# Attention scores of two heads in one matmul: L2's keys in blocks on zero, projected beside the heads

## The chip, the cores and the metric

The kernel runs on one core of a Trainium2 chip. The metric is the device time in microseconds from launch to end of that core. Everything is 32-bit float.

## The reference

A batch of 16 elements, each of 256 tokens by 256 features, goes through four blocks in a row, each steered by a vector `cond` of the element. L0 is a low-rank adapter. L1 is a bidirectional selective state-space layer (512 inner channels, 64 states, a scan over the 256 tokens in each direction) with a gated MLP. L2 and L3 are attention with a feed-forward layer each, L2 with 16 heads of 64 channels, L3 with 16 heads of 16. The change is in L2's attention:

```python
def _attention(x, W_qkv, W_out, b_out):
    qkv = x @ W_qkv
    q, k, v = jnp.split(qkv, 3, axis=-1)          # each (B, 256, 16 heads, 64)
    attn = jnp.einsum('bqhd,bkhd->bhqk', q, k) * DH ** (-0.5)
    attn = jax.nn.softmax(attn, axis=-1)
    out = jnp.einsum('bhqk,bkhd->bqhd', attn, v).reshape(Bq, Tq, INNER)
    return out @ W_out + b_out
```

## The kernel before, in words

The scan of L1 is one loop over 2048 states: 32 units (16 elements, two directions) of 64 states each. For every state, GpSimd (POOL) multiplies the input by a row of B into a buffer `h` (`drive`, L926, four states ahead), ScalarE (ACT) makes the decays (`decay`, L941), VectorE (DVE) scans `h` (`scan`, L969) and TensorE (PE) adds the result up by transposing `h` into `y` (`add_up`, L987, two states behind). The multiplication by a row of C is done by VectorE (L972, with a spread of C made on PE, L956) in five of eight states and by GpSimd (L976) in three of eight. There are eleven buffers `h` (`NH`). GpSimd can only write a buffer once PE has read what was in it.

Beside this loop two generators are advanced. `pend` does the front of the next unit (projections, L393 and L423, softplus, four GpSimd operations L452 to L461) and the back of the unit before, one yield per state. `other` runs `rest(b)`, which is the MLP of L1 and all of L2 and L3 of an element whose scan is done, one or two yields per state, three for two states. The instruction order on each engine is made by the builder, by and large in the order of the program; the engines run their own queues in order. The front and `rest` share two PSUM banks (`bank1`, `bank2`, tag `bank2`).

`rest` of fifteen elements lies beside the loop. For the last element the loop is over: the list `alone` is then filled, `bank2` goes round over six banks, and `rest` runs by itself as the tail of the program.

In L2, `rest` projects q (four times `dense`, two blocks of 128 channels each, L501), then k (the same, copied by ACT at L766), then v (four times at L774). Channels 0 to 63 of a block are an even head, 64 to 127 the odd one. Beside the loop, `heads2` goes over the 16 heads one by one:

- scores, per half of the tokens one matmul with 64 rows and 256 columns (L573);
- the row maximum over both halves (DVE, L578);
- two exponentials with the row sums (ACT, L582);
- one head later, four transposes (L592) and a copy `exT` by ACT (L596);
- for every second head, the product with v (L606) and a copy into `o` (L610).

In the tail, `heads2_alone` does two heads at a time. It puts the scores of the two heads alternately (L626; one head in rows 0 to 63, the other in 64 to 127), and has VectorE copy `exT` (L642).

L3's `heads3` has its keys on two tiles `kd[0]` and `kd[1]` of 128 by 4 by 256, in blocks of 32 rows on zero; small DMAs fill the blocks and the zeros are set once, at the start (L1121).

Weights come in a fixed order (`WEIGHTS`), two tiles in turn; `prefetch` asks for the one after next. All DMAs are issued on SyncE's queue (SP), in order: weights, the rows of B and C for the scan (`bb` of 512 KB for four states, `cb`), and the keys of L3.

Of the kernel before, what the change touches and what calls it, by code (L numbers as in the profile page):

```python
# [15 lines left out]
P = 128  # L16
B, T, D = 16, 256, 256
DC = D // P
# [36 lines left out]
def kernel(ctx: ExitStack, tc: tile.TileContext, a: dict, out: bass.AP):  # L55
# [24 lines left out]
    spill = dram.tile([P, 2, D], F32, name="spill")  # L80
    w3d = dram.tile([P, DC, 1024], F32, name="w3d")
    wvpd = dram.tile([P, 2048], F32, name="wvpd")

    at = {}
    row = 0
# [52 lines left out]
    def chunked(w):  # L138
        return w.rearrange("(c p) f -> p c f", p=P)
# [17 lines left out]
    def halves(t):  # L157
        return t.rearrange("p (c t) -> p c t", c=2)
# [116 lines left out]
    for t in maxima:  # L275
# [11 lines left out]
        )),  # L287
        ("l1w3", lambda w: ((w[:, 0:1024].rearrange("p (c f) -> p c f", c=IC), chunked(a["L1_cond_mlp_w3"])),)),
        ("wq", lambda w: ((w.rearrange("p (c f) -> p c f", c=DC), chunked(a["L2_cond_W_qkv"])[:, :, 0:1024]),)),
        ("wk", lambda w: ((w.rearrange("p (c f) -> p c f", c=DC), chunked(a["L2_cond_W_qkv"])[:, :, 1024:2048]),)),  # L290
        ("wv", lambda w: ((w.rearrange("p (c f) -> p c f", c=DC), chunked(a["L2_cond_W_qkv"])[:, :, 2048:3072]),)),
# [270 lines left out]
        yield  # L562
        prefetch()

    def heads2(q, k, v, o, rows):

        exs, exTs = {}, {}
        for i in range(16 + 3):
            if i < 16:
                sc = halves(bank2("sc"))  # L570
                base, ch = (i % 2) * 64, i // 2
                for t in range(NT):
                    nc.tensor.matmul(  # L573
                        sc[:, t], q[base : base + 64, ch, t * P : (t + 1) * P], k[base : base + 64, ch],
                        start=True, stop=True,
                    )
# [3 lines left out]
                ex = layers["soft"].tile([P, NT, T], F32, name="ex")  # L580
                for t in range(NT):
                    nc.scalar.activation(  # L582
                        ex[:, t], sc[:, t], AF.Exp, bias=nmax[:, t : t + 1],
                        accum_out=rows[:, t, i : i + 1],
                    )
                exs[i] = ex
            if 1 <= i < 17:
                ex = exs.pop(i - 1)
                pt = halves(bank2("pt"))
                for kt in range(NT):  # L590
                    for t in range(NT):
                        nc.tensor.transpose(  # L592
                            pt[:, kt, t * P : (t + 1) * P], ex[:, t, kt * P : (kt + 1) * P], ident
                        )
                exT = layers["soft"].tile([P, NT, T], F32, name="exT", bufs=3)
                nc.scalar.copy(exT, pt)  # L596
                exTs[i - 1] = exT
            yield
            if i % 2 and i >= 3:
                yield  # L600
                po = bank2("po")[:, :T]
                for h in (i - 3, i - 2):
                    exT = exTs.pop(h)
                    base = (h % 2) * 64
                    for kt in range(NT):
                        nc.tensor.matmul(  # L606
                            po[base : base + 64], v[:, kt, h * 64 : (h + 1) * 64], exT[:, kt],
                            start=(kt == 0), stop=(kt == NT - 1),
                        )
                nc.scalar.copy(o[:, (i - 3) // 2], po)  # L610
                yield

    def pair(name):

        return s3.tile([P, IC, T], F32, name=name, tag="h", bufs=NH).rearrange("p (j t) q -> p j t q", j=2)

    def heads2_alone(q, k, v, o, rows):

        exs, exTs = {}, {}
        for i in range(8 + 2):  # L620
            if i < 8:
                scs = [halves(bank2("sc")) for _ in range(2)]
                for t in range(NT):
                    for j in range(2):
                        rw = slice(64 * j, 64 * j + 64)
                        nc.tensor.matmul(  # L626
                            scs[j][:, t], q[rw, i, t * P : (t + 1) * P], k[rw, i], start=True, stop=True
                        )
                nmax = layers["soft"].tile([P, 2, NT], F32, name="nmax2")
                for j in range(2):  # L630
                    nc.vector.tensor_reduce(nmax[:, j], scs[j], AX.X, ALU.max, negate=True)
            if 1 <= i < 9:
                ex = exs.pop(i - 1)
                exT = pair("exT")
                for j in range(2):
                    pt = halves(bank2("pt"))
                    for kt in range(NT):
                        for t in range(NT):
                            nc.tensor.transpose(
                                pt[:, kt, t * P : (t + 1) * P], ex[:, j, t, kt * P : (kt + 1) * P], ident  # L640
                            )
                    nc.vector.tensor_copy(exT[:, j], pt)  # L642
                exTs[i - 1] = exT
            if i >= 2:
                exT = exTs.pop(i - 2)
                po = bank2("po")[:, :T]
                for kt in range(NT):
                    for j in range(2):
                        h = 2 * (i - 2) + j
                        nc.tensor.matmul(  # L650
                            po[64 * j : 64 * j + 64], v[:, kt, h * 64 : (h + 1) * 64], exT[:, j, kt],
                            start=(kt == 0), stop=(kt == NT - 1),
                        )
                nc.scalar.copy(o[:, i - 2], po)
            if i < 8:
                ex = pair("ex")
                for j in range(2):
                    for t in range(NT):
                        nc.scalar.activation(
                            ex[:, j, t], scs[j][:, t], AF.Exp, bias=nmax[:, j, t : t + 1],  # L660
                            accum_out=rows[:, t, 2 * i + j : 2 * i + j + 1],
                        )
                exs[i] = ex

    def heads3(q, k, v, oT):

# [27 lines left out]
        def values(g):  # L694
            ex = []
            for j in range(4):
                tag, n = (("ex", 2), ("exT", 3))[j // 2]
                ex.append(layers["soft"].tile([P, NT, T], F32, name="ex3", tag=tag, bufs=n))
# [31 lines left out]
    def rest(b):  # L730
# [24 lines left out]
        k = layers["pa"].tile([P, 8, T], F32, name="k")  # L755
        v = layers["pa"].tile([P, NT, 1024], F32, name="v")
        o = q
        w = weights("wq", DC)
# [2 lines left out]
            yield  # L761
        prefetch()
        offset(b, 0)
        w = weights("wk", DC)
        for m in range(0, 8, 2):
            nc.scalar.copy(k[:, m : m + 2], dense(w, hT, m, 2, DC))  # L766
# [274 lines left out]
    def late():  # L1041
# [168 lines left out]
```

## Time and profile before

| what | value |
| --- | --- |
| median of three runs | 7628.08 us (7628.05 to 7632.17) |
| the profiled execution, its own time | 7630.37 us |
| its span, first to last instruction | 7628.6 us |
| busy: DVE, POOL | 6886.1 us (90%), 6912.3 us (91%) |
| busy: PE, ACT | 6253.0 us (82%), 5370.7 us (70%) |
| moved by DMA | 675.87 MB, 26.0% of 16 engines' span |
| granted TensorE clock | 0.928 of full speed |

The loop takes nearly all of the span; the tail, the last element alone, begins a little after 7390 us. One element beside the loop takes some 454 us; its L2 heads are 88 us of these, and 26.6 us in the tail. A line of the profile names the line of the kernel, the engine, what is written and read, the count, the busy time and the mean of one, and what the engine waited for before it. A matmul in 32-bit float shows as two records, and records overlap.

### The profile page before, as it was taken

How to read it: one execution, taken by the hardware profiler on the slowest of the kernel's cores; microseconds unless marked ns; L12 is line 12 of the kernel's file. 1: busy time of each engine (PE TensorE's matmuls, PEld its weight loads, DVE VectorE, ACT ScalarE, POOL GpSimd, SP SyncE). 2: the span in 40 equal slices, each digit the busy share in tenths (PEclk: the TensorE clock that was granted, in tenths of full speed). 3: DMA queues.
4: the chain of work that ended last, by engine and by line, in shares of the span. 5: the costliest groups of instructions: out<-in, count | busy, mean ns of one | idle time of the engine just before them, and what ended most of it. 6: DMA issues, size and time to landing. Idle time of an engine off the chain costs nothing. (4 is left out here: it accounts for less than half of the span.)

```text
span 7628.6 us, 100211 instructions
## 1 busy us (share of the span) xinstructions
PE 6253.0 (82%) x35215; PEld 4947.6 (65%) x35215; DVE 6886.1 (90%) x6951; ACT 5370.7 (70%) x12013; POOL 6912.3 (91%) x2991
## 2 busy tenths in 40 slices
PE   6568888888888888888888888888888888888778
PEld 4456666666667666666666667666666666667655
DVE  3988998999999999999999999899999999999972
ACT  3567776777767777776777777777776777777653
POOL 3999999999999999999999999999999999999960
PEclk8679999999999999999999999999999999999999
DMA  4112232222322222232222222222232222222211
GB/s 167 52 60 93 85 103 73 92 90 87 108 79 96 79 95 94 92 103 73 85 100 86 100 86 97 78 92 93 87 105 78 92 85 96 94 92 92 72 64 49
DMA packets 331642, 675.87 MB, mean 89 GB/s; under 512 B 24724, under 2 KB 204032, under 8 KB 326784
## 3 DMA queue, kind: packets, MB, share of 16 engines
q1 hardware_dynamic: 331136, 669.44, 26.0%
q8 instruction: 278, 4.55, 0.2%
q14 instruction: 228, 1.87, 0.1%
HBM read 650.22 MB, written 10.75 MB: 87 GB/s over the span
## 5 line engine op out<-in xcount | busy, mean ns | idle before, releaser
L969 DVE TENSOR_TENSOR_SCAN h<-decay,h 128x512 f32<-128x512 f32 x4096 | 4735.2, 1204 | 271.5 <-ACT decay L941 189.3
L926 POOL TENSOR_TENSOR h<-dtx,bb 128x1024 f32<-128x1024 f32 x2048 | 4794.8, 2370 | 79.9 <-PE y L987 79.8
L987 PE MATMUL y<-ident,h 128*128 128x128 f32 x16384 | 2457.7, 296 | 836.8 <-POOL h L976 798.8
L987 PEld LDWEIGHTS y<-ident,h 128*128 128x128 f32 x16384 | 2083.4, 153 | 1216.4 <-POOL h L976 940.9
L941 ACT ACTIVATE decay<-dt,a_neg_bwd 128x255 f32<-128x255 f32 x4096 | 1814.5, 469 | 824.1 <-DVE h L969 777.0
L941 ACT ACTIVATE decay<-dt,a_neg_fwd 128x255 f32<-128x255 f32 x4096 | 1807.9, 471 | 641.1 <-DVE h L969 598.9
L976 POOL TENSOR_TENSOR h<-h,cb 128x1024 f32<-128x1024 f32 x768 | 1816.5, 2365 | 199.5 <-DVE h L969 172.0
L972 DVE TENSOR_TENSOR h<-h,cs 128x1024 f32<-128x1024 f32 x1280 | 1526.0, 1204 | 73.7 <-PE cs L956 62.9
L956 PE MATMUL cs<-ident,cT 128*128 128x128 f32 x2560 | 503.6, 290 | 88.5 <-DVE h L972 86.1
L956 PEld LDWEIGHTS cs<-ident,cT 128*128 128x128 f32 x2560 | 332.1, 146 | 163.4 <-DVE h L972 123.9
L573 PE MATMUL sc<-k,q 64*128 64x256 f32 x960 | 283.1, 417 | 17.7 <-ACT ex L582 17.0
L393 PE MATMUL pxz<-hTm,w_in 128*128 128x256 f32 x1024 | 275.8, 387 | 15.4 <-DVE maxima L683 12.3
L582 ACT ACTIVATE ex<-sc,nmax 128x256 f32<-128x256 f32 x480 | 222.1, 468 | 71.9 <-DVE nmax L578 69.1
L701 PE MATMUL scT<-qk,kd 128*128 128x256 f32 x984 | 248.8, 385 | 28.6 <-DVE qk L692 23.1
L680 PE MATMUL sc<-kd,qk 128*128 128x512 f32 x490 | 252.0, 621 | 14.2 <-DVE maxima L683 10.0
L596 ACT COPY exT<-pt 128x512 f32<-128x512 f32 x240 | 139.8, 583 | 162.7 <-PE pt L592 162.4
L423 PE MATMUL pdt<-xz,w_dt 128*128 128x256 f32 x1024 | 245.9, 383 | 0.0
L573 PEld LDWEIGHTS sc<-k,q 64*128 64x128 f32 x960 | 167.0, 193 | 99.8 <-ACT ex L582 32.9
L701 PEld LDWEIGHTS scT<-qk,kd 128*128 128x128 f32 x984 | 176.1, 190 | 58.3 <-ACT pr L429 24.9
L393 PEld LDWEIGHTS pxz<-hTm,w_in 128*128 128x128 f32 x1024 | 179.2, 193 | 43.2 <-DVE maxima L683 15.7
L423 PEld LDWEIGHTS pdt<-xz,w_dt 128*128 128x128 f32 x1024 | 189.4, 193 | 21.8
L578 DVE TENSOR_REDUCE nmax<-sc 128x2 f32<-128x512 f32 x240 | 162.1, 676 | 35.7 <-PE sc L573 35.5
(348 smaller groups left out, 7530.1 us busy)
## 6 DMA issues: line engine op xcount, KB each, us to landing
bb<-bd SPq DMA_DIRECT2D x512, 512.0 KB
cb<-bd SPq DMA_DIRECT2D x256, 384.0 KB
l2w<-in_L_cond_W_dram SPq DMA_DIRECT2D x32, 1024.0 KB
l3w<-in_L_cond_W_dram SPq DMA_DIRECT2D x32, 1024.0 KB
l1w<-in_L_cond_mlp_w_dram SPq DMA_DIRECT2D x48, 512.0 KB
w_in<-in_L_cond_fwd_in_w_dram SPq DMA_DIRECT2D x16, 1024.0 KB
w_dt<-_L_cond_fwd_xproj_w_dram SPq DMA_DIRECT2D x16, 1024.0 KB
w_in<-in_L_cond_bwd_in_w_dram SPq DMA_DIRECT2D x16, 1024.0 KB
```

Of the source, the lines that this page charges most:

```text
L393: nc.tensor.matmul(px[:, j], w_in[:, c, (m + j) * P : (m + j + 1) * P], hT[:, c], start=(c == 0), stop=(c == DC - 1),)
L423: nc.tensor.matmul(pp[:, j], w_dt[:, c, (m + j) * P : (m + j + 1) * P], xz[:, c], start=(c == 0), stop=(c == IC - 1),)
L573: nc.tensor.matmul(sc[:, t], q[base : base + 64, ch, t * P : (t + 1) * P], k[base : base + 64, ch], start=True, stop=True,)
L680: nc.tensor.matmul(sc, q[:, g, t * P : (t + 1) * P], kd[g % 2][:, 2 * i : 2 * i + 2], start=True, stop=True)
L701: nc.tensor.matmul(sc[:, kt], kd[g % 2][:, j, kt * P : (kt + 1) * P], q[:, g], start=True, stop=True)
L926: nc.gpsimd.tensor_tensor(h, st[u][4], bb.unsqueeze(1).to_broadcast([P, IC, T]), ALU.mult)
L941: nc.scalar.activation(dc[:, j, 1:T], st[u][3][:, c, when], AF.Exp, scale=a_neg[d][:, c, s : s + 1])
L956: nc.tensor.transpose(cs[:, i % 2, t * P : (t + 1) * P], st[u][1][:, t, s : s + 1].to_broadcast([P, P]), ident)
L969: nc.vector.tensor_tensor_scan(hv, dv, hv, 0.0, ALU.mult, ALU.add)
L972: nc.vector.tensor_tensor(h, h, c.unsqueeze(1).to_broadcast([P, IC, T]), ALU.mult)
L976: nc.gpsimd.tensor_tensor(h, h, c.unsqueeze(1).to_broadcast([P, IC, T]), ALU.mult)
L987: nc.tensor.matmul(ys[u][:, t, c * P : (c + 1) * P], h[:, c, t * P : (t + 1) * P], ident, start=(s == 0 and c == 0), stop=(s == NS - 1 and ...
```

## The change

The projection of k is no longer a stage of its own. `heads2` now also serves the tail, and `heads2_alone` is gone. It goes over 16 steps: a pair of heads `p` and a half of the tokens `t`. Before every second pair it projects two blocks of keys and writes each head's 64 rows into its own columns of `kd`, two copies by ACT. The rest of `kd` is zero, so that one matmul of 128 rows and 512 columns gives the scores of both heads for 128 tokens. One maximum, two exponentials (one per head) and four transposes follow as before; `exT` now holds a pair. As L3 needs zeros in other places of `kd`, both tiles are overwritten with zeros from DRAM before L2 and again after its heads (`blank`, a DMA of 512 KB each). The zeros are written to DRAM once. Weights of v now come before those of k.

```diff
+    def blank(g):
+        nc.sync.dma_start(kd[g], zeros.rearrange("p (j t) -> p j t", j=4))
...
-    def heads2(q, k, v, o, rows):
+    def heads2(w, hT, q, v, o, rows):
         exs, exTs = {}, {}
         for i in range(16 + 3):
+            p, t = i // 2, i % 2
+            if i == 0 or (i % 4 == 2 and i < 14):
+                g = 0 if i == 0 else i // 4 + 1
+                ps = dense(w, hT, 2 * g, 2, DC)
+                keys = kd[g % 2].rearrange("p (m j) t -> p m j t", m=2)
+                for j in range(2):
+                    rw = slice(64 * j, 64 * j + 64)
+                    nc.scalar.copy(keys[rw, :, j], ps[rw])
+                if g == 3:
+                    prefetch()
+                yield
             if i < 16:
+                keys = kd[(p // 2) % 2].rearrange("p (m j) t -> p m j t", m=2)
                 sc = halves(bank2("sc"))
-                base, ch = (i % 2) * 64, i // 2
-                for t in range(NT):
-                    nc.tensor.matmul(
-                        sc[:, t], q[base : base + 64, ch, t * P : (t + 1) * P], k[base : base + 64, ch],
-                        start=True, stop=True,
-                    )
-                nmax = layers["soft"].tile([P, NT], F32, name="nmax")
+                nc.tensor.matmul(sc, q[:, p, t * P : (t + 1) * P], keys[:, p % 2], start=True, stop=True)
+                nmax = layers["soft"].tile([P, 2], F32, name="nmax")
                 nc.vector.tensor_reduce(nmax, sc, AX.X, ALU.max, negate=True)
                 yield
...
             if 1 <= i < 17:
                 ex = exs.pop(i - 1)
+                p1, t1 = (i - 1) // 2, (i - 1) % 2
+                if t1 == 0:
+                    exTs[p1] = layers["soft"].tile([P, 2 * NT, T], F32, name="exT")
+                pt = bank2("pt").rearrange("p (n t) -> p n t", t=P)
+                for n in range(2 * NT):
+                    nc.tensor.transpose(pt[:, n], ex[:, n // NT, (n % NT) * P : (n % NT + 1) * P], ident)
+                (nc.vector.tensor_copy if alone else nc.scalar.copy)(exTs[p1][:, :, t1 * P : (t1 + 1) * P], pt)
...
-    def heads2_alone(q, k, v, o, rows):
...
+        for g in range(2):
+            blank(g)
         hT = yield from norm3(b, m_l2, 0)
...
-        w = weights("wk", DC)
-        for m in range(0, 8, 2):
-            nc.scalar.copy(k[:, m : m + 2], dense(w, hT, m, 2, DC))
-            yield
-        prefetch()
...
-        if alone:
-            heads2_alone(q, k, v, o, rows)
-        else:
-            yield from heads2(q, k, v, o, rows)
+        yield from heads2(weights("wk", DC), hT, q, v, o, rows)
+        yield
+        for g in range(2):
+            blank(g)
...
-            nc.gpsimd.memset(kd[j], 0.0)
+            if j == 0:
+                nc.gpsimd.memset(kd[j], 0.0)
+                nc.sync.dma_start(zeros, kd[j].rearrange("p j t -> p (j t)"))
```

More of the change, by code (lines that the diff above doesn't have):

```diff
@@ L82 @@
     wvpd = dram.tile([P, 2048], F32, name="wvpd")
+    zeros = dram.tile([P, 4 * T], F32, name="zeros")
     at = {}
@@ L289 @@
         ("wq", lambda w: ((w.rearrange("p (c f) -> p c f", c=DC), chunked(a["L2_cond_W_qkv"])[:, :, 0:1024]),)),
+        ("wv", lambda w: ((w.rearrange("p (c f) -> p c f", c=DC), chunked(a["L2_cond_W_qkv"])[:, :, 2048:3072]),)),
         ("wk", lambda w: ((w.rearrange("p (c f) -> p c f", c=DC), chunked(a["L2_cond_W_qkv"])[:, :, 1024:2048]),)),
-        ("wv", lambda w: ((w.rearrange("p (c f) -> p c f", c=DC), chunked(a["L2_cond_W_qkv"])[:, :, 2048:3072]),)),
         ("l2out", lambda w: ((w.rearrange("p (c f) -> p c f", c=8), chunked(a["L2_cond_W_out"])),)),
@@ L563, in feed_forward @@
         prefetch()
-    def heads2(q, k, v, o, rows):
+    def blank(g):
+        nc.sync.dma_start(kd[g], zeros.rearrange("p (j t) -> p j t", j=4))
+    def heads2(w, hT, q, v, o, rows):
         exs, exTs = {}, {}
         for i in range(16 + 3):
+            p, t = i // 2, i % 2
[9 more added lines that the diff above has]
+                yield
             if i < 16:
+                keys = kd[(p // 2) % 2].rearrange("p (m j) t -> p m j t", m=2)
                 sc = halves(bank2("sc"))
-                base, ch = (i % 2) * 64, i // 2
-                for t in range(NT):
-                    nc.tensor.matmul(
-                        sc[:, t], q[base : base + 64, ch, t * P : (t + 1) * P], k[base : base + 64, ch],
-                        start=True, stop=True,
-                    )
-                nmax = layers["soft"].tile([P, NT], F32, name="nmax")
+                nc.tensor.matmul(sc, q[:, p, t * P : (t + 1) * P], keys[:, p % 2], start=True, stop=True)
+                nmax = layers["soft"].tile([P, 2], F32, name="nmax")
                 nc.vector.tensor_reduce(nmax, sc, AX.X, ALU.max, negate=True)
                 yield
-                ex = layers["soft"].tile([P, NT, T], F32, name="ex")
-                for t in range(NT):
+                ex = layers["soft"].tile([P, 2, T], F32, name="ex")
+                for j in range(2):
                     nc.scalar.activation(
-                        ex[:, t], sc[:, t], AF.Exp, bias=nmax[:, t : t + 1],
-                        accum_out=rows[:, t, i : i + 1],
+                        ex[:, j], sc[:, j], AF.Exp, bias=nmax[:, j : j + 1],
+                        accum_out=rows[:, t, 2 * p + j : 2 * p + j + 1],
                     )
@@ L588, in heads2 @@
                 ex = exs.pop(i - 1)
[L589 to L597, printed above, removed]
+                p1, t1 = (i - 1) // 2, (i - 1) % 2
[5 more added lines that the diff above has]
+                (nc.vector.tensor_copy if alone else nc.scalar.copy)(exTs[p1][:, :, t1 * P : (t1 + 1) * P], pt)
             yield
@@ L601, in heads2 @@
                 po = bank2("po")[:, :T]
-                for h in (i - 3, i - 2):
-                    exT = exTs.pop(h)
-                    base = (h % 2) * 64
+                p1 = (i - 3) // 2
+                exT = exTs.pop(p1)
+                for j in range(2):
+                    h = 2 * p1 + j
                     for kt in range(NT):
                         nc.tensor.matmul(
-                            po[base : base + 64], v[:, kt, h * 64 : (h + 1) * 64], exT[:, kt],
+                            po[64 * j : 64 * j + 64], v[:, kt, h * 64 : (h + 1) * 64], exT[:, j * NT + kt],
@@ L608, in heads2 @@
                             start=(kt == 0), stop=(kt == NT - 1),
                         )
-                nc.scalar.copy(o[:, (i - 3) // 2], po)
+                nc.scalar.copy(o[:, p1], po)
                 yield
-    def pair(name):
-        return s3.tile([P, IC, T], F32, name=name, tag="h", bufs=NH).rearrange("p (j t) q -> p j t q", j=2)
-    def heads2_alone(q, k, v, o, rows):
[L619 to L663, printed above, removed]
@@ L696, in values @@
             for j in range(4):
-                tag, n = (("ex", 2), ("exT", 3))[j // 2]
-                ex.append(layers["soft"].tile([P, NT, T], F32, name="ex3", tag=tag, bufs=n))
+                if j < 2:
+                    ex.append(layers["soft"].tile([P, NT, T], F32, name="ex3", tag="ex"))
+                elif j == 2:
+                    two = layers["soft"].tile([P, 2 * NT, T], F32, name="ex3", tag="exT")
+                    ex += [two[:, :NT], two[:, NT:]]
                 sc = halves(bank2("scT"))
@@ L751, in rest @@
         prefetch()
+        for g in range(2):
+            blank(g)
         hT = yield from norm3(b, m_l2, 0)
         q = layers["pa"].tile([P, 8, T], F32, name="q")
-        k = layers["pa"].tile([P, 8, T], F32, name="k")
         v = layers["pa"].tile([P, NT, 1024], F32, name="v")
```

## Prediction, made before the changed kernel was run

> **What bounds the kernel now.** I read the page first, then busy time by stage, then who waited for whom in the stage that the change touches, then single instructions there and in the tail.
>
> ```profile
> PE 6253.0 (82%) x35215; PEld 4947.6 (65%) x35215; DVE 6886.1 (90%) x6951; ACT 5370.7 (70%) x12013; POOL 6912.3 (91%) x2991
> ...
> L969 DVE TENSOR_TENSOR_SCAN h<-decay,h 128x512 f32<-128x512 f32 x4096 | 4735.2, 1204 | 271.5 <-ACT decay L941 189.3
> L926 POOL TENSOR_TENSOR h<-dtx,bb 128x1024 f32<-128x1024 f32 x2048 | 4794.8, 2370 | 79.9 <-PE y L987 79.8
> ...
> L573 PE MATMUL sc<-k,q 64*128 64x256 f32 x960 | 283.1, 417 | 17.7 <-ACT ex L582 17.0
> ...
> L680 PE MATMUL sc<-kd,qk 128*128 128x512 f32 x490 | 252.0, 621 | 14.2 <-DVE maxima L683 10.0
> ```
>
> POOL (L926, L976) and VectorE (L969) carry the scan. POOL idles for little, and where it does, the multiply L926 waits for PE's transposes into y, which free an h buffer. POOL's work is not touched, so the loop gets shorter only where POOL idles less. One batch element as an example (46 us of L2's q, k, v; 88 us of its heads; the rest), then the two stages of the last element, which runs alone:
>
> ```profile
> 2012.00:2058.00 46.00, 42.82 (x225) 33.89 (x224) 39.91 (x37) 42.59 (x86) 41.40 (x18) 1.00 0.48 169
> 2058.00:2146.00 88.00, 70.97 (x446) 55.28 (x446) 80.56 (x79) 62.19 (x175) 87.55 (x39) 0.91 0.19 65
> 2146.00:2411.00 265.00, 224.61 (x1280) 178.08 (x1277) 253.52 (x262) 189.79 (x406) 250.48 (x109) 0.95 0.26 86
> 7416.00:7459.80 43.80, 39.18 (x138) 29.02 (x138) 3.54 (x6) 14.84 (x24) 0.00 (x0) 0.86 0.28 96
> 7459.80:7486.40 26.60, 25.38 (x193) 16.50 (x192) 20.39 (x33) 17.93 (x72) 0.00 (x0) 1.00 0.12 40
> ```
>
> Columns: stretch, length, busy PE, PEld, DVE, ACT, POOL, clock, DMA share, GB/s. In the heads POOL is full (87.55 of 88) and the others have room. In q, k, v it is the reverse: PE and ACT are at 93% and POOL loses 4.6 us. In the tail's heads PE is full (25.38 of 26.60). Who held POOL, in the waits of 2012 to 2146 and in POOL's, ACT's and PE's instructions in order of time:
>
> ```profile
> POOL h L926 <- PE y L987: 5.1, 3, 2.8
> ```
> ```profile
> 2046.83 2.37 POOL L926 TENSOR_TENSOR h<-dtx,bb 128x1024 f32<-128x1024 f32 x1 [2.78 <-PE y L987]
> ...
> 2055.68 2.36 POOL L926 TENSOR_TENSOR h<-dtx,bb 128x1024 f32<-128x1024 f32 x1 [1.83 <-PE y L987]
> 2058.49 2.36 POOL L926 TENSOR_TENSOR h<-dtx,bb 128x1024 f32<-128x1024 f32 x1 [0.45 <-PE y L987]
> 2060.80 2.36 POOL L976 TENSOR_TENSOR h<-h,cb 128x1024 f32<-128x1024 f32 x1
> ```
> ```profile
> 2044.64 1.99 PE L501 MATMUL dense<-hT,wk 128*128 128x256 f32 x8 [1.65 <-ACT k L766]
> ...
> 2051.12 3.60 PE L774 MATMUL pv<-wv,hT 128*128 128x512 f32 x8
> 2054.56 1.04 PE L987 MATMUL y<-ident,h 128*128 128x128 f32 x8
> ...
> 2058.55 1.13 PE L573 MATMUL sc<-k,q 64*128 64x256 f32 x4
> ```
> ```profile
> 7459.79 0.48 PE L626 MATMUL decay<-k,q 64*128 64x256 f32 x1
> 7459.79 0.48 PE L626 MATMUL sc<-k,q 64*128 64x256 f32 x1
> 7460.11 0.38 PE L626 MATMUL decay<-k,q 64*128 64x256 f32 x1
> 7460.11 0.38 PE L626 MATMUL sc<-k,q 64*128 64x256 f32 x1
> ```
>
> The transposes stand behind the twelve projections of q, k, v on PE's queue; and PE itself waits 1.65 us for a PSUM bank that ACT has yet to empty.
>
> **The change, part by part.** An f32 matmul leaves two records.
>
> *Scores in the loop.* By mean durations a pair of heads would fall from 8 x 417 = 3.3 us to 4 x 621 = 2.5 us. These overlap, so they are not costs. A head's four records of 256 columns span 1.13 us with the last at 0.38, so starts are some 0.21 to 0.25 apart; at L774, of 512 columns too, 8 records span 3.60 with the last at 0.59, so 0.43 apart. Per pair: 8 x 0.21 = 1.7 us before, 4 x 0.43 = 1.7 us after. Cost and gain 0: half of the new products are with zeros.
>
> *Where a rule speaks against it.* In the tail, records of the two heads start in the same hundredth (7459.79, 7459.79) and again 0.32 and 0.21 later: rows 0 to 63 and 64 to 127 work at once. The Trainium skill ("TensorE: Matmul & The Clock Gate", Part 3 on packing small matmuls) says that a matmul with few rows takes as long as one with 128, and that such matmuls in different row groups run at once; filling the rows with zeros throws that away. By the rule everywhere it would be 128 pairs x 0.85 = 109 us of PE. The loop's rows show four matmul records of one head alone, one after another, so nothing is lost there; I charge the tail only.
>
> *Tail.* Before: 3.1 us per pair of heads (scores begin at 7464.27, 7467.37, 7470.47, ...), of which 1.06 are scores. After: 1.71 + the same 2.04 = 3.75, so 8 x 0.65 = +5.2 us. The four key projections (7445.71 to 7452.61, 6.9 us) move and stay on PE: 0. Before the first score come two copies of the keys on ACT, 2 x 0.58 = 1.2, partly filled by the next projection: +1. The half-pair order leaves less between a score and its transposes: from a score's start to its second exponential's end it is 1.0 + 0.7 + 0.9 + hand-overs of 0.1 = 3.0 us, while PE has 0.85 + 0.5 + 0.85 = 2.2 without an output matmul between: bound 0 to 0.8 us per pair, 0 to 6; by the 0.3 us that L639 waits per pair now I take 2. Tail: **+8 us** (5 to 13).
>
> *Keys moved in the loop.* Four projections (8 records in some 1.73 us each, 6.9 in all) leave the stage where PE holds POOL and go into the heads, one before every second pair. Cover there: PE 71.0 + 6.9 of 88. If that cover were gone, they would cost what they cost now. In q, k, v, v takes k's place, so PE's work up to 2046.8 is as before and the wait of 2.78 stays. After it, PE has one key projection, two scores and a set of transposes (1.7 + 2.0 + 0.4 = 4.1 us) where v's four had 6.9; the 1.83 and 0.45 should go: 2.3 us. Late next is ACT: from 2048.7 to 2061.6 it has no gap (dtx to uu, 6.4 us, four copies of v 2.3), VectorE waits 3.0 for a decay, and L976 at 2060.80 began 0.3 us after its scan. In the new order two key copies, two exponentials and one exT (1.2 + 0.9 + 0.6) stand there for v's copies. So POOL, earlier, will wait for a scan instead; bound 0 to 2.3, I take half: **-1.1 us** per element, 15 elements, **-16 us**.
>
> *Copies on ACT.* A group of keys is written as two copies of 64 rows x 512 where one of 128 x 512 took 0.58; the row nearest is that one, and with the columns equal I take 0.58: +2.3 us per element. From below 0.3 each (rows counted) they would be free. Cover: ACT 62.2 of 88. Behind a copy that waits for its projection stand the decays, and VectorE for those; at the first group the score itself waits for the copies, and the y transposes stand behind it on PE. Charged 0 beyond what is above; without cover 15 x 2.3 = +35.
>
> *The blanks.* Four DMAs of 512 KB per element, on SP's queue, in front of bb, cb and weights. The page has 669 MB in 26% of the span: 3.0 us per MB, an estimated 1.6 us for each. A bb is asked for when its buffer comes free and used four multiplies later (9.5 us); L926 waited for PE in 79.8 of its 79.9 us, never for a DMA. Two blanks before a bb (3.1 us) stay under 9.5. What a blank waits for (the scores of the last pair, L3 of the element before) is three or more steps old. 0; if not covered, 6 us per element.
>
> *Rest.* The zero fill of one block (0.95 us on POOL) goes, before the loop, where POOL then idles 36.9 us: 0. One more turn of the generator per element moves all after it by two thirds of a state, 2.4 us, and adds no work; the last but one element ends at 7388 with the loop at 7392: 0. exT and ex sizes are the same in sum; l2w1 is fetched later, still some 25 us ahead of its use: 0.
>
> **Sum:** +8 - 16 = -8 on 7630.4 (the profiled execution; span 7628.6), 7622. That execution is 2.3 above the median of the three, 7628.1, so about **7620**.
>
> **The rivals.**
> 1. *No measurable change*, the sum above, 7600 to 7640 (within 15 us, 0.2%, about what a measurement can tell from none, for most of it). For it: POOL is full in the heads, the score's PE time is equal. Chance 0.42.
> 2. *All of POOL's wait for y goes*, as ACT keeps up: 5.1 x 15 = 76 less, 8 more: 7560. For: that wait is PE's. Against: the first 2.78 lies before the change of order. Chance 0.21.
> 3. *The keys block PE in the heads.* In the loop two PSUM banks serve scores, transposes, projections and the front's matmuls. Each projection waits for a bank that ACT must empty (1.65 us at 2044.64), in front of y. Four such waits, 6.6 us per element, less the two now seen in q and k (2.6): 4 x 15 = 60, with 8 for the tail 7696; half of it 7660. It decides once PE's lateness uses up the free h buffers, so that POOL waits for y within the heads. For: PE is in order, and ACT waits 11.8 us for transposes there already. Against: POOL shows almost no wait in these 88 us. Chance 0.37.
>
> That the matmuls get no cheaper is already in the sum; that the blanks delay bb is part of 3's upper end.
>
> **Numbers.** Faster by over 0.2%: nearly all of 2 and a quarter of 1: 0.30. Within: 0.32 from 1 and the edges. Slower: 3: 0.38. Range 7575 to 7690: half of 2 and the top of 3 left out.
>
> **What would show it.** L573 and L626 gone, score records of 128x512 at about 0.6 us; POOL's waits for y after v gone (right) or new ones inside the heads (rival 3); PE busy in a heads stage up by about 7 us, POOL full; the tail's heads with keys some 8 us longer than 6.9 + 26.6. L926 waiting for bb, or POOL less than 95% busy in the heads, would make it wrong.

## The result, and the profile after

The changed kernel is slower: a median of 7729.8 us (7723.2 to 7735.2, four runs) against 7628.1 us (7625.5 to 7632.2), a ratio of 1.013 with a 95% interval of 1.0118 to 1.0142. That is about 100 us more, where 8 us less had been forecast, and outside the range. The profiled execution took 7727.3 us, its span is 7725.5 us.

From the page of the changed kernel, the lines that answer to those of before. L885 is now POOL's multiply `drive`, L928 the scan, L935 POOL's multiplication by C, L589 L2's scores; L640 and L664 are L3's scores and their transposed counterpart.

```profile
PE 6169.6 (80%) x34703; PEld 4804.0 (62%) x34703; DVE 6886.6 (89%) x6951; ACT 5475.3 (71%) x12077; POOL 6911.8 (89%) x2990
...
L928 DVE TENSOR_TENSOR_SCAN h<-decay,h 128x512 f32<-128x512 f32 x4096 | 4746.0, 1211 | 291.1 <-ACT decay L900 163.9
L885 POOL TENSOR_TENSOR h<-dtx,bb 128x1024 f32<-128x1024 f32 x2048 | 4794.1, 2369 | 160.7 <-PE y L946 159.0
...
L664 PE MATMUL scT<-qk,kd 128*128 128x256 f32 x984 | 264.9, 401 | 83.1 <-DVE qk L652 65.1
...
L589 PE MATMUL sc<-kd,q 128*128 128x512 f32 x492 | 280.0, 653 | 26.9 <-ACT exT L608 16.3
...
L640 PE MATMUL sc<-kd,qk 128*128 128x512 f32 x490 | 255.9, 615 | 43.9 <-DVE maxima L643 43.8
```

Read the busy times first. POOL works 6911.8 us, before 6912.3; VectorE 6886.6, before 6886.1. So the 97 us of span are idle time of both. The wait of `drive` for PE's transposes into `y` has doubled, 79.9 to 160.7. And the two rows whose waits have grown most on PE are not L2's: they belong to L3. The change leaves L3's instructions as they are; it only gives the exponentials of `values` other buffers (two of a group's four heads share one), and the first two experiments show that this costs nothing. L640 waited 14.2 before and waits 43.9 now. L664 stood as L701 in the page before:

```profile
L701 PE MATMUL scT<-qk,kd 128*128 128x256 f32 x984 | 248.8, 385 | 28.6 <-DVE qk L692 23.1
```

Busy time by stage, after, for the element that the prediction took as its example, with the columns as there: q and v, then the heads with their keys, then the stage of L3's attention. The last two lines are the tail's two stages.

```profile
2027.00:2063.70 36.70, 33.11 (x169) 25.31 (x168) 35.47 (x34) 33.52 (x72) 32.41 (x15) 1.00 0.48 156
2063.70:2161.00 97.30, 79.64 (x483) 58.42 (x482) 84.68 (x83) 75.57 (x195) 95.76 (x42) 0.93 0.27 91
2268.90:2379.00 110.10, 96.88 (x548) 71.99 (x547) 104.33 (x108) 81.48 (x172) 100.42 (x44) 0.97 0.26 84
7509.10:7545.80 36.70, 32.06 (x104) 23.10 (x105) 3.54 (x6) 12.67 (x20) 0.00 (x0) 0.84 0.25 86
7545.80:7584.90 39.10, 38.45 (x193) 22.71 (x193) 21.35 (x33) 23.54 (x81) 0.00 (x0) 1.00 0.24 81
```

The stage of L3's attention of the same element before:

```profile
2249.90:2355.00 105.10, 95.91 (x551) 71.64 (x551) 103.51 (x108) 79.03 (x171) 100.42 (x44) 0.98 0.24 83
```

q, v and the heads take 36.7 + 97.3 = 134.0 us; q, k, v and the heads took 46.0 + 88.0 = 134.0. The changed part is neither faster nor slower in this element. L3's stage does the same work (POOL 100.42 us in 44 instructions both times) and takes 5.0 us longer: POOL idles 9.7 us of it where it idled 4.7. Averaged over fourteen elements in the middle of the loop, POOL idles 28.2 us per element against 21.6 before; 15 times the difference is 99 us. The loss is in the loop, and most of it is not where the change is.

Who held POOL in L3's stage, after and then before (each line: waits in total, times, longest):

```profile
POOL h L885 <- PE y L946: 7.2, 4, 3.8
POOL h L935 <- DVE h L928: 2.5, 1, 2.5
```
```profile
POOL h L976 <- DVE h L969: 2.9, 3, 1.3
POOL h L976 <- POOL h L926: 1.0, 1, 1.0
POOL h L926 <- PE y L987: 0.7, 1, 0.7
```

The longest wait, 3.78 us at 2331.77, and what PE did before it, in order of time:

```profile
2323.33 4.67 POOL L885 TENSOR_TENSOR h<-dtx,bb 128x1024 f32<-128x1024 f32 x2
2331.77 2.37 POOL L885 TENSOR_TENSOR h<-dtx,bb 128x1024 f32<-128x1024 f32 x1 [3.78 <-PE y L946]
```
```profile
2322.97 0.44 PE L651 MATMUL pm<-ident,maxima 128*128 128x128 f32 x2 [1.26 <-ACT pr L430]
2323.25 1.04 PE L946 MATMUL y<-ident,h 128*128 128x128 f32 x8
2324.12 0.38 PE L915 MATMUL cs<-ident,cT 128*128 128x128 f32 x2
2327.12 1.10 PE L664 MATMUL scT<-qk,kd 128*128 128x256 f32 x4 [2.62 <-DVE qk L652]
2328.06 1.89 PE L424 MATMUL pdt<-xz,w_dt 128*128 128x256 f32 x8
2329.79 1.03 PE L664 MATMUL scT<-qk,kd 128*128 128x256 f32 x4
2330.65 1.04 PE L946 MATMUL y<-ident,h 128*128 128x128 f32 x8
```

At the same place in the kernel before:

```profile
2303.24 0.38 PE L691 MATMUL pm<-ident,maxima 128*128 128x128 f32 x2
2303.45 1.25 PE L987 MATMUL y<-ident,h 128*128 128x128 f32 x10
2306.26 1.97 PE L701 MATMUL scT<-qk,kd 128*128 128x256 f32 x8 [1.55 <-DVE qk L692]
2308.06 0.82 PE L987 MATMUL y<-ident,h 128*128 128x128 f32 x6
```

In L3 PE spreads the maxima (`pm`), VectorE adds them to `qk`, and PE makes `scT` from it. PE is in order. Before, the chain came up with transposes in front of it, and 4.6 us lie between the starts of two groups of `y`. After, `pm` first waits 1.26 us for a PSUM bank that ACT must empty (`pr`, of the next unit's front), then `scT` 2.62 us for VectorE, and a product `pdt` of the front follows; the two groups of `y` start 7.4 us apart. POOL's buffer is late by 3.8 us. L3 and the next unit's front are the same instructions as before. What differs is how they lie against each other and against the scan: L3 comes later by one turn of the generator.

The example stands for the others. Over the fourteen elements, POOL waits for `y` in L3 for 7.3 us per element; before it was 0.3. A second, smaller growth lies where a forward unit starts: there POOL's `yg` (L470, in the back of the unit before) waits for VectorE for 4.0 us per element, before 2.4.

### The profile page after: what moved, and what is told of

It reads as the page before. It is cut to its first block, busy times and chain, and to the rows that moved or that the text cites. A ratio compares the mean times of both kernels' runs of the same rounds, so it can differ in the third digit from the quotient of the medians.

```text
span 7725.5 us, 99391 instructions
## 1 busy us (share of the span) xinstructions
PE 6169.6 (80%) x34703; PEld 4804.0 (62%) x34703; DVE 6886.6 (89%) x6951; ACT 5475.3 (71%) x12077; POOL 6911.8 (89%) x2990
## 5 line engine op out<-in xcount | busy, mean ns | idle before, releaser
L928 DVE TENSOR_TENSOR_SCAN h<-decay,h 128x512 f32<-128x512 f32 x4096 | 4746.0, 1211 | 291.1 <-ACT decay L900 163.9
L885 POOL TENSOR_TENSOR h<-dtx,bb 128x1024 f32<-128x1024 f32 x2048 | 4794.1, 2369 | 160.7 <-PE y L946 159.0
L946 PE MATMUL y<-ident,h 128*128 128x128 f32 x16384 | 2361.0, 288 | 733.9 <-POOL h L935 684.4
L946 PEld LDWEIGHTS y<-ident,h 128*128 128x128 f32 x16384 | 2008.6, 148 | 1152.8 <-POOL h L935 796.1
L900 ACT ACTIVATE decay<-dt,a_neg_bwd 128x255 f32<-128x255 f32 x4096 | 1837.3, 472 | 813.2 <-DVE h L928 757.6
L935 POOL TENSOR_TENSOR h<-h,cb 128x1024 f32<-128x1024 f32 x768 | 1815.5, 2364 | 187.7 <-DVE h L928 177.1
L664 PE MATMUL scT<-qk,kd 128*128 128x256 f32 x984 | 264.9, 401 | 83.1 <-DVE qk L652 65.1
L589 PE MATMUL sc<-kd,q 128*128 128x512 f32 x492 | 280.0, 653 | 26.9 <-ACT exT L608 16.3
L640 PE MATMUL sc<-kd,qk 128*128 128x512 f32 x490 | 255.9, 615 | 43.9 <-DVE maxima L643 43.8
L664 PEld LDWEIGHTS scT<-qk,kd 128*128 128x128 f32 x984 | 182.2, 198 | 122.1 <-issue 69.9
L618 PE MATMUL po<-exT,v 128*64 128x256 f32 x992 | 170.7, 425 | 31.2 <-ACT ex L595 30.7
L470 POOL TENSOR_TENSOR yg<-yg,xz 128x1024 f32<-128x1024 f32 x32 | 75.2, 2351 | 112.8 <-DVE yg L1128 112.8
```

The lines of the kernel that those rows point to most:

```text
L589: nc.tensor.matmul(sc, q[:, p, t * P : (t + 1) * P], keys[:, p % 2], start=True, stop=True)
L640: nc.tensor.matmul(sc, q[:, g, t * P : (t + 1) * P], kd[g % 2][:, 2 * i : 2 * i + 2], start=True, stop=True)
L664: nc.tensor.matmul(sc[:, kt], kd[g % 2][:, j, kt * P : (kt + 1) * P], q[:, g], start=True, stop=True)
L885: nc.gpsimd.tensor_tensor(h, st[u][4], bb.unsqueeze(1).to_broadcast([P, IC, T]), ALU.mult)
L900: nc.scalar.activation(dc[:, j, 1:T], st[u][3][:, c, when], AF.Exp, scale=a_neg[d][:, c, s : s + 1])
L928: nc.vector.tensor_tensor_scan(hv, dv, hv, 0.0, ALU.mult, ALU.add)
```

## The experiments

All ratios are against the kernel before on the same chip, with 95% intervals; the runs of one section share a chip, and different sections may not. A "turn" is one bare `yield` in `rest`: it adds no instruction and sends everything of `rest` behind it to a later place in the order, two thirds of a state on. "Wait for `y` in L3" is POOL's, averaged over the fourteen elements as above.

### The turn alone, taken out and put in

The changed `rest` ends L2's heads with one more turn than the old one. The theory was that this turn carries the loss, the rivals that the keys, the blanks or the tail do.

```diff
         yield from heads2(weights("wk", DC), hT, q, v, o, rows)
-        yield
```


> The changed kernel without the one extra generator turn (a bare yield) after L2's heads; all else as changed. Theory A (the extra turn moves L3 against the front of the next unit, so that PE's wait for the shifted queries falls in front of projections and y): L3 is back in its old place, the 6 us per element that the second unit of each element lost go, some 7640 to 7650. Theory B (the keys beside the heads make L3 late by themselves, or the blanks do): 7715 to 7730, as changed.

```diff
 # in the kernel before
         else:
             yield from heads2(q, k, v, o, rows)
+        yield
```


> The kernel before with one bare yield added after the heads beside the loop, and nothing else. Theory A: L3 moves as in the changed kernel and POOL waits for y there; 7690 to 7720. Theory B: the turn adds no work, 7625 to 7635.

Without the turn the changed kernel takes 7617.2 us, 0.9991 (0.9984 to 0.9998). The kernel before with the turn takes 7741.5 us, 1.0156 (1.0139 to 1.0173). The turn is the loss, in either kernel. The rows of the page show the same signature come and go. First the changed kernel without the turn, then the kernel before with it:

```profile
L884 POOL TENSOR_TENSOR h<-dtx,bb 128x1024 f32<-128x1024 f32 x2048 | 4795.2, 2372 | 73.4 <-PE y L945 73.1
...
L664 PE MATMUL scT<-qk,kd 128*128 128x256 f32 x984 | 250.1, 387 | 29.0 <-DVE qk L652 23.1
...
L640 PE MATMUL sc<-kd,qk 128*128 128x512 f32 x490 | 252.4, 622 | 14.1 <-DVE maxima L643 10.2
```
```profile
L927 POOL TENSOR_TENSOR h<-dtx,bb 128x1024 f32<-128x1024 f32 x2048 | 4792.2, 2367 | 187.1 <-PE y L988 186.2
...
L701 PE MATMUL scT<-qk,kd 128*128 128x256 f32 x984 | 267.8, 405 | 84.1 <-DVE qk L692 65.4
...
L680 PE MATMUL sc<-kd,qk 128*128 128x512 f32 x490 | 255.9, 615 | 43.6 <-DVE maxima L683 43.5
```

PE's waits in L3, 23.1 and 10.2 us without the turn, are 65.4 and 43.5 with it, whichever way L2 is written. POOL's wait for `y` in L3 goes with them: 0.3 us per element without the turn, 7.2 with it. What held POOL in that stage of the example element, in the same order:

```profile
POOL h L934 <- DVE h L927: 3.1, 4, 1.3
POOL h L934 <- POOL h L884: 1.0, 1, 1.0
```
```profile
POOL h L927 <- PE y L988: 7.2, 4, 3.8
POOL h L977 <- DVE h L970: 2.5, 1, 2.5
```

### The blanks alone

```diff
 # in the kernel before: the zeros written once, and per element
+        for g in range(2):
+            blank(g)
 # ahead of L2 and again behind its heads
```


> The kernel before with the four zero fills of 512 KB per element added at the changed kernel's two places (and the write of the zeros to DRAM); the heads are as before, L3's keys are written after the fills. Theory A: the fills are covered, 7625 to 7640. Theory C (fills delay bb or L3's keys on SP's queue): 7660 to 7720, with POOL's multiply waiting for bb or PE waiting for the keys of L3.

7622.5 us, 0.9996 (0.9988 to 1.0005). Four DMAs of 512 KB per element on SP's queue cost nothing that shows.

### The tail alone

The changed kernel, whose last element projects its keys ahead and uses the old `heads2_alone`.

```diff
+        if alone:
...
+            heads2_alone(q, k, v, o, rows)
+        else:
+            yield from heads2(weights("wk", DC), hT, q, v, o, rows)
```


> The changed kernel, but the last element, alone, has the old pairwise heads with 64 rows per score and its keys projected before them. If the tail carries what the spans show (the time behind the last scan is 239.5 before and 244.8 changed): 5 us less than changed, about 7722 to 7726; by my prediction of the tail 8 less. If the tail's loss is not from row pairing: within 2 us of changed.

7725.2 us, 1.0131 (1.0116 to 1.0146): the loop's loss stays. In the trace the last element goes from its first q projection to L2's output projection in 61.0 us in the changed kernel, in 55.6 before, and in 55.5 here. So the tail costs 5.4 us, and the old heads give it back. That is read from the traces: 5.4 us are 0.07% of the whole, less than the intervals of the ratios tell apart.

### Which work it is that must not be late

Give the turn back at the end of L2's feed-forward, so that L3 is in its old place again; or, in the kernel without the turn, put it only behind L3's heads.

```diff
     def feed_forward(b, up, dn, hT, bup, r, turns=2):
...
-        yield
-        yield
+        for _ in range(turns):
+            yield
...
             b, "l2w1", "l2w2", hT, "L2_cond_b1", 1, 1
```


> The changed kernel, turn included, but L2's feed-forward, just ahead of L3, ends with one bare yield instead of two: the heads and L2's output stay one turn late, L3 is back in its old turn. Theory P (the turn costs by where L3's attention meets the front of the next unit): 7615 to 7640, no wait for y above 3 us in the second unit. Theory Q (the turn costs in L2's output and feed-forward): 7700 or more.

```diff
 # in the kernel without the turn
         yield from heads3(q, k, v3, oT)
         yield
+        yield
```


> The changed kernel without the turn after the heads, and with one bare yield after L3's attention instead: the same number of turns per element, but only L3's end is late. Theory P: 7615 to 7650 (at most the 1.7 us per element that the next unit's start waits for VectorE, 25). Theory N (the number of turns itself costs, since an element then runs past the end of its second unit): 7700 to 7730.

L3 in place: 7652.4 us, 1.0033 (1.0021 to 1.0044). Only what follows L3 late: 7637.9 us, 1.0014 (1.0007 to 1.0021). The first lies between the two expectations, nearer to that for L3's place (7615 to 7640); the second is as expected for it. From 1.013 to 1.0033 is 0.97%, some 74 us: most of the loss hangs on L3's place, though the wait for `y` in L3 does not go wholly with it (3.3 us per element are left of 7.3). Between 1.0033 and 0.9991 are 0.42%, some 32 us, for L2's output projection and feed-forward being late; the turn behind L3's heads alone costs 0.23%, some 18 us of the 74 if the parts add up.

### Is it a matter of the phase?

If one turn were bad because L3 then falls on an unlucky phase of the front or of the scan's pattern, other numbers of turns should be good again. Three bare yields behind the heads:

```diff
         yield from heads2(weights("wk", DC), hT, q, v, o, rows)
         yield
+        yield
+        yield
```


> The changed kernel with three bare yields after the heads instead of one: L3 comes two whole states later than without any, with the same alignment of single and double turns. If the alignment of odd and even states is what costs: 7615 to 7640. If it is the place against the front (theory P): no return, 7680 to 7760, since L3's waits meet the front's projections at least as long.

And a theory that L3's place against the front's `pdt` alone decides: the changed kernel with the front of the forward units later by one yield ahead of `pdt` too.

```diff
         pr = s1.tile([P, IC, T], F32, name="pr")
+        if d == 0:
+            yield
```


> The changed kernel, turn included, with one bare yield in the front of each forward unit before its second projection (pdt): that projection comes one state later, as L3 did by two thirds of one. Theory P (relative place): most of the 100 us are gone, 7620 to 7660. If L3 were late by itself, without the front: 7715 to 7740.

Three turns: 7751.5 us, 1.0158 (1.0138 to 1.0178). Front later: 7738.6 us, 1.0144 (1.0124 to 1.0164). Neither brings anything back; the theory of the place against `pdt` fell.

### Is it the wait for VectorE's addition?

PE's wait for `qk` had grown the most. The shift that makes it (`pm` and the addition) can be issued inside the group of heads before, after its third score, so that `scT` finds it done.

```diff
-            yield from values(g)
-            shifted(g + 1)
+            for n, _ in enumerate(values(g)):
+                if n == 2:
+                    shifted(g + 1)
+                yield
             yield
```


> The changed kernel, turn included, but in L3 the shift of the next group's queries (pm and the addition on VectorE) is given out inside the group before it, after its third score, instead of right before its own scores; no turn more or less. Theory S (the turn costs because PE stands 2.6 and 1.9 us before L3's scores for that addition, queued on VectorE behind two scans, with y behind it): the wait is gone and with it the 4 to 5 us per element at states 100 to 104, 7655 to 7680; the 2 us at the start of the next unit stay. Theory R (the front and L3 together are too much for PE there, whatever the order): 7715 to 7740.

7736.0 us, 1.0143 (1.0128 to 1.0158). The wait for VectorE is gone and the time is not: this theory fell as well, and POOL's wait for `y` in L3 is still 7.2 us per element. The time lies where the other theory put it (7715 to 7740): L3 and the front together are too much for PE there, whatever the order. That this is so is not shown; the stage of L3 has PE busy for 95.91 of 105.1 us already before. The page shows what came instead:

```profile
L887 POOL TENSOR_TENSOR h<-dtx,bb 128x1024 f32<-128x1024 f32 x2048 | 4799.4, 2376 | 174.1 <-PE y L948 171.8
...
L664 PE MATMUL scT<-qk,kd 128*128 128x256 f32 x976 | 269.1, 405 | 88.9 <-ACT ex L667 60.8
```

`scT` idles PE for 88.9 us as before (83.1), but now for ACT, that is for one of the two PSUM banks: the exponential `ex` has yet to empty it. A part of its order of time, some 3700 us in:

```profile
3712.75 1.13 PE L664 MATMUL scT<-qk,kd 128*128 128x256 f32 x4 [0.82 <-ACT ex L667]
...
3717.62 1.13 PE L664 MATMUL scT<-qk,kd 128*128 128x256 f32 x4 [0.93 <-ACT ex L667]
```

### Old heads in the tail, without the turn, and the early shift

If the parts are what they seem, the best version has the new heads in the loop, no extra turn and the old heads in the tail. The early shift (the edit of the last section) was tried on it and on the kernel before.

```diff
 # changed kernel, without the turn
+        if alone:
...
+            heads2_alone(q, k, v, o, rows)
+        else:
+            yield from heads2(weights("wk", DC), hT, q, v, o, rows)
-        yield
```


> The changed kernel without the turn and with the old pairwise heads for the last element alone: the two parts of the change that help in the loop, without the two that cost. From the runs so far: without the turn 0.9991 of before, 5 to 6 us less for the tail: 0.9983 to 0.9985, some 13 us less than before. If the parts do not add up: 0.999 or more.

> The kernel of the last run with the earlier shift in L3 as well. Theory S: the 1.6 us for which PE stands on that addition in the second group go too, up to 1.5 us per element, 10 to 25 us less than without it. Theory R: the same within 8 us.

> The kernel before with the earlier shift in L3 alone. Theory S: 10 to 25 us less than before, as in the run before this one. Theory R: the same within 8 us.

The best version takes 7597.1 us (7589.0 to 7610.0), 0.9961 (0.9946 to 0.9976): faster than both kernels. The early shift makes both slower, which neither theory expected: 7635.6 us, 1.0008 (0.9999 to 1.0016), and 7711.9 us, 1.0108 (1.0093 to 1.0123). So the last section is fairly read with the shift on both sides: with it the turn still costs 1.0143 against 1.0008, about 1.3% when the tail is taken off, nearly as much as without it (1.4%). In the kernel before, POOL's idle time per element rises from 21.6 to 27.3 us with it, most of the rise in the first half of the element's forward unit, far from L3: as with the turn, an edit that adds no work moves waits in places that it does not touch. The gain of the best version is larger than its terms: 7617.2 less 5.4 would be 7612. In the loop its instruction order is that of the kernel without the turn on every engine, so no change of order explains the remaining 15 us, and they stay open; the runs of the kernel without the turn, on another chip, reached from 7603 to 7633.

### Is it the bank that `pdt` holds?

`pdt` keeps one of two banks over two yields, and ACT empties it behind the second. If the competition for banks is the cause, a bank taken per 128 channels and emptied at once should make the turn cheap.

```diff
-        for m in range(0, IC, 2):
-            pp = halves(bank1("pdt"))   # two blocks, a yield behind each, then two activations
+            # for each block:
+            pp = bank1("pdt")[:, :T]    # one block, its activation, a yield
```

With the turn, and without it:

> The changed kernel, turn included; the front's second projection (pdt) takes a PSUM bank for each 128 channels and ACT empties it at once, where one bank was held for two of them over two states. Same instructions and turns. Theory K (in the turn's place L3's scores and pdt compete for the two banks, and PE stands in front of y): 7640 to 7680, 50 us or more below the changed kernel, and within 50 of the next run. Theory L (the place is bad whatever the banks): 7715 to 7750.

> The same in the changed kernel without the turn. Theory K: there is little competition here, 7600 to 7630. Theory L: 7600 to 7640, some 100 below the run before this one.

7714.0 us, 1.0115 (1.0095 to 1.0134), and 7645.1 us, 1.0025 (1.0015 to 1.0036). The theory of the bank expected 7640 to 7680 with the turn; 7714.0 is the time of the other one. The turn costs 0.9% here where it costs 1.4% with the long-held bank, but most of that difference, 0.34%, comes from the second kernel itself being slower than its counterpart (0.9991). POOL's wait for `y` in L3 is 6.8 us per element with the turn and 0.7 without it, where it was 7.3 and 0.3. So the long hold of the bank is at most a small part of the cause.

### How wide is the good place?

One bare yield fewer than without the turn (one of the two ahead of `pnorm` taken out), and two bare yields behind the heads:

```diff
 # without the turn, ahead of pnorm
         yield
-        yield
```
```diff
 # with the turn
         yield from heads2(weights("wk", DC), hT, q, v, o, rows)
         yield
+        yield
```


> The changed kernel without the turn and with one of the two bare yields ahead of the normalisation of L2's heads left out as well: all from there on one turn earlier than in the kernel before. If the kernel before sits in a narrow best place: 7650 to 7720. If one turn later is a bad place among good ones: 7600 to 7640.

> The changed kernel with two bare yields after the heads instead of one. Narrow best place: 7720 to 7760. One bad place: below 7680, though three turns gave 7751.

7614.1 us, 0.9985 (0.9978 to 0.9992), and 7749.1 us, 1.016 (1.014 to 1.018). With the others this makes a row, in turns beside the place of the kernel before:

| turns | -1 | 0 | +1 | +2 | +3 |
| --- | --- | --- | --- | --- | --- |
| ratio | 0.9985 | 0.9991 | 1.0130 | 1.0160 | 1.0158 |
| POOL idle, us per element | 19.7 | 21.1 | 28.2 | 29.3 | 29.7 |
| of it, wait for `y` in L3 | 0.7 | 0.3 | 7.3 | 2.9 | 2.3 |

In time it is a step between 0 and +1, not a narrow best place: in this window, earlier costs nothing, and later costs nearly all of it at once. The last row says that it is not one wait. At +2 and +3 the wait for `y` in L3 is less than half of what it is at +1, and POOL's multiplication by C waits more instead: in the stretch from 1000 to 6000 us 147.6 and 158.2 us for scans (115.8 at +1), and 57.0 and 37.6 us for nothing that the profile shows.

## Why the prediction was wrong

It failed in one term, under "Rest": "One more turn of the generator per element moves all after it by two thirds of a state, 2.4 us, and adds no work; the last but one element ends at 7388 with the loop at 7392: 0." The turn costs 1.4%, measured by taking it out of one kernel and putting it into the other. The argument looked only at the end of the row (does the last element still come in time?) and at the work added (none). It did not ask what else the moved work would then stand beside: L3 and the next unit's front share two PSUM banks and PE's one queue, and POOL waits for what comes behind them. In place of the 0, the turn brought 7 us of POOL's waiting for `y` in L3 per element (0.3 to 7.3) and 1.6 us more at the start of the next forward unit; other waits fell by some 1.5, so that POOL's idle time rose by 7.1 (21.1 to 28.2). The term was also given without bounds, though the trace of before could not show L3 in another place. In the same paragraph, "exT and ex sizes are the same in sum" is not so (five tiles of 512 columns before, six after), but no run shows a cost of it.

The other terms together were forecast at -8 us. The changed kernel without the turn is that sum measured: 0.9991, or -7 us with an interval of -1.5 to -12. That the sum comes out is in part luck, as the terms show. Point by point:

- **Scores in the loop, 0.** Right. In the trace a score of 512 columns keeps PE for 0.86 us, 0.43 for each record, as in the prediction; the example element's two stages take 134.0 us as before.
- **The rule on small matmuls.** These traces agree with it: a record of 256 columns takes 0.38 us with 64 rows (L626 before) as with 128 (L501). The place that was chosen for it was right: the tail alone lost the concurrency of two row groups, and it lost 5.4 us there. In the loop nothing of the 109 us that the rule would have given everywhere is seen.
- **The tail, +8 (5 to 13).** The mechanism was right, the size was the low end: +5.4. Scores begin 0.86 us apart where they follow each other (the trace below), and from one key projection (7559.37) to the next (7568.67), two pairs later, lie 9.3 us, of which the projection takes 1.83: 3.7 per pair, near the 3.75 worked out. 8 times 0.65 is already 5.2, so the two added items, +1 for the first copies and +2 for the order of half pairs, came to next to nothing.

```profile
7553.17 1.02 PE L589 MATMUL sc<-kd,q 128*128 128x512 f32 x2
7554.03 1.04 PE L589 MATMUL decay<-kd,q 128*128 128x512 f32 x2
7554.91 0.60 PE L607 MATMUL decay<-ident,ex 128*128 128x128 f32 x4
```

- **Keys moved out of q, k, v, -16.** The direction was right; the size is not settled. In the profiled executions the loop ends 7.5 us earlier without the turn and 38 us earlier in the best version, whose loop has the same order; 16 lies between. From q to the end of the heads (states 16 to 63 of an element) POOL idles 6.6 us before, 5.9 without the turn and 4.6 in the best version, that is 0.7 to 2.0 less, where 1.1 had been forecast. In the example element POOL's waits for y fell from three (5.1 us) to one (3.8), and what was named as "late next" came and took the gain back there: POOL waits for scans. In the changed kernel's waits for this stretch:

```profile
POOL h L885 <- PE y L946: 3.8, 1, 3.8
POOL h L935 <- DVE h L928: 2.9, 2, 2.5
```

- **ACT's copies, 0 in time.** Right: 0.58 us for 64 rows by 512 (median of the eight copies in the example), the upper end of its bounds; in the loop no cost of it shows.
- **The blanks, 0.** Right: the blanks alone gave 0.9996.

Of the rivals, the third gave times (7660 to 7696) nearest to the result, but not for its reason: it held that the keys would block PE within the heads. POOL is busy 95.76 of 97.3 us there, and the same heads without the turn lose nothing. Its picture, an in-order PE that waits for a bank which ACT has to empty with transposes behind it, is a part of what the trace shows in L3 (1.26 us ahead of `pm`), where no rival looked; the longer wait there, 2.62 us, is for VectorE.

What stays open is why the step lies just between 0 and +1. Waits for VectorE's addition were taken away and others took their place; a shorter hold of one bank took the wait for `y` in L3 from 7.3 to 6.8 us. That PE simply has too much to do where L3 and the front lie together is a rival that no run excludes. A third shared bank would be a direct test of the banks; it was not run. What is shown is the cause in the program (the turn), the stage that mostly pays (L3 beside the next unit's front), and, for one turn, the chain through which it pays (PE's waits, then `y`, then POOL); with two and three turns more of the waiting is for scans. Which shared resource sets the limit there is not shown. The clock is no part of it: its mean is 0.936 in the slower kernel's profile and 0.928 before.

## What to carry to other kernels

A line that adds no instruction can cost more than all that a change adds and removes: count every shift of order as an edit, and list for each piece of work that it moves which queues and buffers it will now meet in whose company. When a page's growth is in rows that the change did not touch, compare stages of equal work in both traces, then take out the shift alone and put it alone into the old kernel; two runs settled here what 97 us of idle time did not say. And when a wait is removed and the time stays, look at the same instruction's next releaser before believing in either wait, and read it against a kernel that has the same edit without the shift.

## What the hardware showed that was not expected

Two heads in two row groups run together with hardly a loss: in the tail the old form's pair of scores takes 1.06 us against 1.71 for the filled blocks, and eight times that difference, 5.2 us, would be nearly all of the tail's 5.4. An ACT copy of 64 rows costs what one of 128 rows does, 0.58 us at 512 columns. Both were within bounds; the surprise was the scan's loop, in which a delay of 2.4 us in one generator, once per element, becomes about 7 us of idle POOL per element (21.6 to 28.2, and 21.6 to 29.0 with the turn alone).
